# A decoder kernel: softmax left undivided until after the projection, and queries by seven products in thirty groups instead of sixteen

## The chip, the cores and the metric

The kernel runs on one core of one Trainium2 chip. TensorE (PE) multiplies matrices into PSUM[...]; VectorE (DVE) and ScalarE (ACT) read PSUM and work on SBUF; GpSimd (POOL) works on SBUF; SyncE (SP) issues most of the DMAs, ACT and POOL some. The metric is the device time of one execution in microseconds (us). Where several runs are compared, their median is given.

## The reference

Four batches of 512 rows pass through two layers, all in fp32. Most of the work, and all of the change, is in the attention of the second layer, with 16 heads of width 128, queries from the rows `x` (width 512) and keys and values from a context (width 256):

```
q = (hidden_states @ Wq).reshape(B, Sq, H, D)
k = (encoder_hidden_states @ Wk).reshape(B, Skv, H, D)
v = (encoder_hidden_states @ Wv).reshape(B, Skv, H, D)
q = rmsnorm(q, gq)
k = rmsnorm(k, gk)
scores = jnp.einsum('bqhd,bkhd->bhqk', q, k) * scale
attn = jax.nn.softmax(scores, axis=-1)
out = jnp.einsum('bhqk,bkhd->bqhd', attn, v)
out = out.reshape(B, Sq, H * D)
return out @ Wo
...
x = x + jnp.tanh(g_xattn[1]) * _L1_xattn_ref(_layernorm(x, axis=-1), ctx_1024, ...)
x = x + jnp.tanh(g_ffn[1]) * _L1_ffn_ref(_layernorm(x, axis=-1), ...)
```

Before it stand a smaller attention and a linear layer (layer 0). After it comes a layer of 16 experts, of which each row uses four; it applies to the first batch alone.

## The kernel before, in words

Layer 0 runs first, for all batches. Then the attention of the second layer runs as 64 steps, one for each head and batch: step `i` belongs to group `m = i // 2`, and a group is two heads of one batch, so there are 32 groups, eight to a batch. The experts' work for the first batch is laid into steps 22 to 56, beside the attention of later batches. I call these the expert steps.

A step has four quarters, and each begins with one score matmul: 128 queries against 512 keys (`scores`, L968). Around it `step` (from L1301) lists the other pieces of each quarter by hand:

- `keys_values` (L776) of the next group, in the even step: eight matmuls of 512 columns.
- the queries of the next group. `queries` (L858) makes a head with four matmuls of 512 columns, so eight for a group. `quarter_queries` (L881) makes both heads at once, as a 2 x 2 block product by seven block products in place of eight: fourteen matmuls of 256 columns, and sums on DVE (L896 to L918). It needs sums of blocks of `Wq` (`combine` in `load_wq`, L731 to L734, on POOL, once a group) and of the rows (`combine_rows`, L748 to L751, on DVE, once a batch). `SWITCH = (12, 28)` gives the groups that are made so.
- `values` (L1015) of the head two steps back: four matmuls of 512 columns, into the one bank psO, which ACT copies to `oT` (L1022).
- `project` (L1066): for a group, four chunks of 128 rows, each the sum over its two heads of `oT` times `wo`, so eight matmuls of 512 columns. Each chunk fills one bank (psA, psO, psT, psA), and DVE adds it to `x_sb`, times a gate (`add_to_x`, L276).

The softmax of a score tile goes: DVE multiplies by the scale of the queries and takes the row extreme (L982); ACT exponentiates and sums the rows (L983); DVE inverts the sum (L989) and multiplies the tile by it (L990), both in `share`; DVE transposes it in blocks of 32 (L261) into `tP`. After a head's fourth tile, sixteen DMAs on SP move `tP` to `big` (`move_probs`, L269), which `values` reads two steps later.

Keys take a way of their own: ACT squares them, DVE and POOL scale them (L806, L193, L810), DVE transposes blocks (L821), ACT's queue writes them to DRAM (L828) and reads them back in place (L836) as `kT`. The sums of squares of the queries go through DVE (L939), a small matmul (L947), DVE and POOL to `rq`, which L982 needs.

Each engine runs its instructions in the order of the program. That order is written by hand: a piece emits its matmuls at once, `tick()` counts them (a matmul of 512 columns is one), and `later(n, f)` emits `f` once `n` more are counted. So an instruction that waits holds up all that follows on its engine. Tiles come from pools of a few buffers in turn; PSUM has three buffers psA, two psS (scores), two psT and one psO, and a new tile waits until the last reader of the buffer's former tile is done. DMAs wait, in the same way, for the DMA that last used the same completion counter.

Of the kernel before, what the change touches and what calls it, by code (L numbers as in the profile page):

```python
# [15 lines left out]
P = 128  # L16
# [39 lines left out]
def tile_gated_decoder(  # L56
# [87 lines left out]
        nc.sync.dma_start(t[:, :, 1, :], wv_v[:, :, cols(m)])  # L144
        wkv_of[m] = t

    wqk0 = work.tile([P, G, DM], F32, tag="wo", name="wqk0")
    wq0, wk0 = (wqk0[:, a, 0 : CC * D].rearrange("p (c d) -> p c d", c=CC) for a in (0, 1))
    nc.sync.dma_start(wq0, wq0_d.rearrange("(c p) d -> p c d", p=P))
    load_ctx(0)  # L150
    nc.sync.dma_start(wk0, wk0_d.rearrange("(c p) d -> p c d", p=P))
# [71 lines left out]
        return [lambda c=c: chunk(c) for c in range(NC)], stats  # L223

    def normalised(b, c, mv, rs):
        xn = row("y", 2)
        nc.vector.tensor_scalar(
            xn, x_sb[:, b * NC + c, :], mv[:, c, 0:1], rs[:, c : c + 1], ALU.subtract, ALU.mult
        )
        return xn  # L230
# [187 lines left out]
    def layer0_attention():  # L418
# [56 lines left out]
                load_ctx(b)  # L475

        load_wq(0)()
        load_wo(0)
        load_wo(1)
        first_rows = turned_rows(0, lx1, lnt)  # L480
        for b in range(NB - 1):
            for c in range(NC):
# [224 lines left out]
    turned, moved, ends = {}, {}, {}  # L707
    n_heads = G * len(groups)

# [253 lines left out]
    def scores(i, c):  # L963


        m, h = divmod(i, G)
        sc = ps_s()
        nc.tensor.matmul(  # L968
            sc, q_of[m][h][:, c * P : (c + 1) * P], k_of[m][:, :, h, :], start=True, stop=True
        )  # L970
        st = {}

        def top():
            scale = rq_of[m][:, h * NC + c : h * NC + c + 1]

            st["e"] = row("prob", 3)
            st["den"] = col(1, "den")
# [5 lines left out]
            nc.scalar.activation(  # L983
                st["e"], st["e"], AF.Exp, bias=top, scale=-1.0, accum_out=st["den"]
            )

        def share():
            rden = col(1, "rden")
            nc.vector.reciprocal(rden, st["den"])  # L989
            nc.vector.tensor_scalar(st["e"], st["e"], rden, None, ALU.mult)  # L990
# [12 lines left out]
        later(0, top)  # L1003
        later(2, share)
        later(3, turn)

    def values(i):

        m, h = divmod(i, G)
        if h == 0:  # L1010
            o_of[m] = work.tile([P, G, S], F32, tag="oT", name="oT")
        v, oT, pT = v_of[m], o_of[m], moved.pop(i)
        po = ps_o()
        for k in range(NC):
            nc.tensor.matmul(  # L1015
                po, v[:, k, h * D : (h + 1) * D], pT[:, :, k, :], start=(k == 0), stop=(k == NC - 1)
            )
            tick()

        def copy():  # L1020

            nc.scalar.copy(  # L1022
                oT[:, h, :].rearrange("p (c g r) -> p c g r", c=NC, r=TB),
                po.rearrange("p (g c r) -> p c g r", c=NC, r=TB),
            )

        later(0, copy)
# [13 lines left out]

    def end_values(c):
        m, h = divmod(n_heads - 1, G)
        po = ps_a()
# [6 lines left out]
        later(0, lambda: nc.scalar.copy(o_of[m][:, h, c * P : (c + 1) * P], po[:, 0:P]))  # L1051

    def project(m, chunks):

        b, g = groups[m]
        oT, wo = o_of[m], wo_of[m]

        def add(t, pp):
            add_to_x(t, pp, tg[:, 1:2])
            if g == NG - 1 and b > 0:  # L1060
                nc.sync.dma_start(out_v[:, t, :], x_sb[:, t, :])

        for c in chunks:
            pp = (ps_a, ps_o, ps_t, ps_a)[c]()
            for j in range(G):
                nc.tensor.matmul(  # L1066
                    pp, oT[:, j, c * P : (c + 1) * P], wo[:, j, :], start=(j == 0), stop=(j == G - 1)
                )
# [104 lines left out]
            tick()  # L1173

    def keep_rows(s, st, table):
        y = row("y", 2)
        nc.vector.tensor_copy(y, st["py"])
        nc.sync.dma_start(table[s * P : (s + 1) * P, :], y)

# [32 lines left out]

    def rows_of(table, c, k):

        yg = row("y", 2)
# [60 lines left out]
    put(last, 3, count_over)  # L1276
    for c in range(NC):
        for k in range(TOPK):
            put(last + 1 + (c * TOPK + k) // 3, (c * TOPK + k) % 3, lambda c=c, k=k: add_row(c, k))
    for b in range(1, NB):  # L1280
        i = (b - 1) * NG * G + NG
        for j, f in enumerate(turned_rows(b, lx1, lnt)):
            put(i + j // NC * (1 + j % NC), 3 if j >= NC else j, f)
        if (b + 1) * NG > SWITCH[0]:
            put(2 * max(b * NG, SWITCH[0]) - 2, 1, lambda b=b: combine_rows(b))
        if b > 1:
            put(i, 3, lambda b=b: load_ctx(b))

# [9 lines left out]
    for c in (2, 3):  # L1298
        put(0, c - 1, lambda c=c: linear(NB - 1, turned0[NB - 1], [c]))

    def step(i):  # L1301
        m, h = divmod(i, G)
        q = m + 1
        late, late_before = by_quarters(q), by_quarters(m)
        pieces = [[], [], [], []]
        if i >= G:
            pieces[0 if i == n - 1 or h and late else 2].append(lambda: values(i - G))
        if i == n - 1:
            pieces[1].append(lambda: project(m - 1, [0, 1]))
            pieces[2] += [lambda: project(m - 1, [2, 3]), lambda: end_turn(0)]  # L1310
            pieces[3] += [lambda: values(i - 1), lambda: end_turn(1)]
            pieces[3] += [lambda: end_values(0), lambda: end_turn(2), lambda: end_values(1)]
            pieces[3] += [lambda: project(m, [0]), lambda: end_turn(3), lambda: end_values(2)]
            pieces[3] += [lambda: project(m, [1]), lambda: end_values(3)]
            pieces[3] += [lambda: project(m, [2]), lambda: project(m, [3])]
        if h == 0:
            if 0 < m < M - 1:
                pieces[0].append(lambda: keys_values(q, [0, 1]))
                pieces[1].append(lambda: keys_values(q, [2, 3]))
            if m + 2 < M:  # L1320
                pieces[2 if late else 3].append(lambda: load_wkv(m + 2))
            if m >= 2 and not late_before:
                pieces[3].append(lambda: project(m - 2, [2, 3]))
                pieces[3].append(lambda: later(4, lambda: load_wo(m)))
            if late and q < M:
                pieces[3].append(lambda: quarter_queries(q, 0))
        elif i < n - 1:
            if q < M and not late:
                pieces[0].append(lambda: queries(q, 0))
            if q < M:  # L1330
                pieces[1].append(lambda: (quarter_queries if late else queries)(q, 1))
            if m + 2 < M:
                pieces[2].append(lambda: later(6, load_wq(m + 2)))
            if late:
                pieces[2].append(lambda: project(m - 1, [0, 1]))
            if m >= 1:
                pieces[3].append(lambda: project(m - 1, [2, 3] if late else [0, 1]))
            if late and q < M:
                pieces[3].append(lambda: later(2, lambda: load_wo(q)))
            if m == 0:  # L1340
                pieces[3].append(lambda: tick(8))
        for quarter in range(4):
            if i < n:
                scores(i, quarter)
# [76 lines left out]
```

## Time and profile before

| | |
|---|---|
| median of 3 runs | 1434.96 us (1433.12 to 1439.84) |
| the profiled execution | 1437.51 us |
| its span | 1435.7 us |
| granted TensorE clock | 0.998 |
| instructions | 14871 |
| DMA | 226.99 MB, mean 158 GB/s |
| chain that ended last | PE 82%, DVE 8%, ACT 3%, DMA 2% |

In what follows a row of the timeline gives start and duration in us, the engine, the line, the operation, what it writes and reads, and how many instructions were merged; a bracket tells for how long the engine was idle before it, and what ended that. `PE` is the matmuls and `PEld` the loads of weights. A fp32 matmul appears as two records. The ends of matmuls are modelled, so the distance from one start to the next is the better measure of what one costs. A row of a group gives busy time, the mean of one in ns, and after the second bar the idle time before. A row of the windows gives busy time and count for PE, PEld, DVE, ACT and POOL, then the granted clock, the busy share of the DMA engines and GB/s.

### The profile page before, as it was taken

The numbers are of one execution on the slowest core, as the hardware profiler recorded it, in microseconds if no ns is written. First come the engines' busy times: TensorE is split into PE (matmuls) and PEld (weight loads), VectorE is DVE, ScalarE is ACT, GpSimd is POOL, SyncE is SP. The second block draws the span as 40 slices with busy tenths as digits, with TensorE's granted clock in tenths as the row PEclk, the third lists the DMA queues.
The fourth block names the chain that finished last, engine by engine and source line by source line (L and its number), as shares of the span: only waits on it lengthen the run. The fifth ranks groups of instructions, "written<-read, shape, count | busy, mean of one in ns | idle before, by whom it ended". The sixth has DMA issues, their size and how long they took to land.

```text
span 1435.7 us, 14871 instructions
## 1 busy us (share of the span) xinstructions
PE 1408.4 (98%) x3937; PEld 703.1 (49%) x3937; DVE 936.2 (65%) x2216; ACT 574.7 (40%) x1708; POOL 332.9 (23%) x274
## 2 busy tenths in 40 slices
PE   8999998999999999999999999999999999999998
PEld 4554443444444444555555555554555555544434
DVE  4778766767666677655666655566656565667774
ACT  5652224444444444333443334344334344434431
POOL 2324315322111112212221212221221222012320
PEclk9999999999999999999999999999999999999999
DMA  7533026545444445455565665656565666555652
GB/s 258 175 127 123 1 66 181 147 138 136 132 133 140 133 143 172 154 170 177 173 168 174 205 210 147 187 174 178 176 188 151 191 205 183 162 154 167 194 148 83
DMA packets 155356, 226.99 MB, mean 158 GB/s; under 512 B 24576, under 2 KB 90640, under 8 KB 155264
## 3 DMA queue, kind: packets, MB, share of 16 engines
q1 hardware_dynamic: 127312, 177.86, 42.1%
q10 hardware_dynamic: 23040, 33.56, 7.3%
q0 software_dynamic: 4912, 14.53, 3.7%
q8 instruction: 35, 0.57, 0.2%
q14 instruction: 57, 0.47, 0.1%
HBM read 129.62 MB, written 30.17 MB: 111 GB/s over the span
## 4 chain that ended last, share of the span: by engine, by line
PE 82%; DVE 8%; ACT 3%; DMA 2%; issue 1%; POOL 1%; SPq 1%; ACTq 0%; POOLq 0%
PE psA L776 15%; PE psS L968 13%; PE psO L1015 13%; PE psA L858 7%; PE psA L1066 6%; PE psA L881 5%; PE psA L1141 5%; PE psT L1066 3%; PE psO L1066 3%; PE psA L364 3%; PE psA L1169 2%; PE psA L695 1%; DMA kT<-k_d 1%; DVE x_sb L276 1%; ACT prob L983 1%
## 5 line engine op out<-in xcount | busy, mean ns | idle before, releaser
L983 ACT ACTIVATE prob<-prob,top 128x512 f32<-128x512 f32 x256 | 184.6, 721 | 562.5 <-DVE prob L982 524.1
L968 PE MATMUL psS<-kT,qT 128*128 128x512 f32 x512 | 262.3, 596 | 5.0 <-DVE x_sb L276 2.8
L776 PE MATMUL psA<-wkv,ctx 128*128 128x512 f32 x512 | 231.8, 593 | 0.3 <-ACT v L771 0.3
L1015 PE MATMUL psO<-big,v 128*128 128x512 f32 x504 | 228.9, 596 | 0.0
L982 DVE TENSOR_SCALAR_CACHE_REDUCE prob<-psS,rq 128x512 f32<-128x512 f32 x256 | 188.0, 736 | 28.9 <-PE psS L968 18.5
L989 DVE RECIPROCAL rden<-den 128x1 f32<-128x1 f32 x256 | 41.5, 162 | 242.2 <-ACT prob L983 232.9
L261 DVE STREAM_TRANSPOSE tP<-prob 128x512 f32<-128x512 f32 x252 | 178.7, 709 | 6.5
L193 POOL TENSOR_TENSOR rq<-qss,mhalf 128x8 f32<-128x8 f32 x32 | 53.4, 1668 | 485.3 <-DVE qss L955 485.3
L1015 PEld LDWEIGHTS psO<-big,v 128*128 128x128 f32 x504 | 96.0, 191 | 119.8 <-issue 115.5
L776 PEld LDWEIGHTS psA<-wkv,ctx 128*128 128x128 f32 x512 | 96.3, 190 | 118.1 <-issue 109.6
L990 DVE TENSOR_SCALAR prob<-prob,rden 128x512 f32<-128x512 f32 x256 | 141.3, 552 | 9.0
L968 PEld LDWEIGHTS psS<-kT,qT 128*128 128x128 f32 x512 | 92.9, 190 | 79.6 <-issue 62.0
L193 POOL TENSOR_TENSOR rk<-kss,mhalf 128x8 f32<-128x8 f32 x32 | 52.8, 1650 | 319.3 <-DVE kss L806 319.2
L1066 PE MATMUL psA<-wo,oT 128*128 128x512 f32 x256 | 121.1, 594 | 2.2 <-ACT oT L1022 2.2
L858 PE MATMUL psA<-lnT,wq 128*128 128x512 f32 x256 | 115.6, 592 | 0.0
L1141 PE MATMUL psA<-gu,xgT 128*128 128x352 f32 x272 | 86.0, 459 | 0.0
L821 DVE STREAM_TRANSPOSE tK<-kn 128x256 f32<-128x256 f32 x128 | 45.4, 411 | 55.3 <-POOL kn L810 55.3
L1066 PEld LDWEIGHTS psA<-wo,oT 128*128 128x128 f32 x256 | 48.1, 190 | 64.2 <-issue 54.4
L858 PEld LDWEIGHTS psA<-lnT,wq 128*128 128x128 f32 x256 | 48.3, 190 | 59.3 <-issue 59.3
L796 ACT ACTIVATE ksq<-kn 128x128 f32<-128x128 f32 x256 | 75.2, 298 | 0.0
L1141 PEld LDWEIGHTS psA<-gu,xgT 128*128 128x128 f32 x272 | 51.7, 190 | 37.9 <-issue 15.5
L276 DVE SCALAR_TENSOR_TENSOR x_sb<-psA,tg,x_sb 128x512 f32<-128x512 f32 x80 | 58.2, 727 | 6.7 <-PE psA L695 3.8
(197 smaller groups left out, 1811.5 us busy)
## 6 DMA issues: line engine op xcount, KB each, us to landing
big<-tP SPq DMA_DIRECT2D x1008, 64.0 KB
k_d<-tK ACTq DMA_DIRECT2D x32, 512.0 KB
kT<-k_d ACTq DMA_DIRECT2D x128, 128.0 KB
wq<-in_wq_dram SPq DMA_DIRECT2D x32, 512.0 KB
wo<-in_wo_dram SPq DMA_DIRECT2D x32, 512.0 KB
gu<-in_gate_dram SPq DMA_DIRECT2D x16, 704.0 KB
gu<-in_up_dram SPq DMA_DIRECT2D x16, 704.0 KB
wkv<-in_wk_dram SPq DMA_DIRECT2D x32, 256.0 KB
```

Source lines behind the costliest of these rows:

```text
L193: nc.gpsimd.tensor_tensor(out, v, mhalf[:, :n], ALU.pow)
L261: nc.vector.transpose(tP[:, :, c, :], e.rearrange("p (j r) -> p j r", r=TB))
L776: nc.tensor.matmul(pp, ctxs[b][:, k, c * P : (c + 1) * P], wkv[:, k, :, :].rearrange("p a n -> p (a n)"), start=(k == 0), stop=(k == CC - 1),)
L796: nc.scalar.activation(sq[:, c, at], kn[:, c, at], AF.Square, accum_out=st["kss"][:, c * G + h : c * G + h + 1],)
L858: nc.tensor.matmul(pp, wq[:, k, h * D : (h + 1) * D], lx1[b][:, k, :], start=(k == 0), stop=(k == KC - 1))
L968: nc.tensor.matmul(sc, q_of[m][h][:, c * P : (c + 1) * P], k_of[m][:, :, h, :], start=True, stop=True)
L982: nc.vector.tensor_scalar(e, x, scale, 3.0e38, ALU.mult, ALU.min, accum_out=top)
L983: nc.scalar.activation(st["e"], st["e"], AF.Exp, bias=top, scale=-1.0, accum_out=st["den"])
L990: nc.vector.tensor_scalar(st["e"], st["e"], rden, None, ALU.mult)
L1015: nc.tensor.matmul(po, v[:, k, h * D : (h + 1) * D], pT[:, :, k, :], start=(k == 0), stop=(k == NC - 1))
L1066: nc.tensor.matmul(pp, oT[:, j, c * P : (c + 1) * P], wo[:, j, :], start=(j == 0), stop=(j == G - 1))
L1141: nc.tensor.matmul(st[a][:, :FF], st["xgT"][:, k * P : (k + 1) * P], st["gu"][:, a, k, :], start=(k == 0), stop=(k == KC - 1),)
```

## The change

It has two parts, and moves pieces around them.

The exponentials are not divided any more. `den` becomes a column of `dens`, one tile of four columns for a head; when its four tiles are through, `part` takes the four reciprocals at once and multiplies by the gate, which gives `share_of[i]`. `project` now works on one head and one chunk: a single matmul, whose result is added to `x_sb` times `share_of[i]` where it was `tg` before. The last two heads are still divided and projected together.

`SWITCH` becomes `(2, 32)`: the queries of groups 2 to 31 are made by `quarter_queries`.

To this belongs: `wo` and `oT` are held and loaded by head; `project` of head `i - 3` runs in step `i`, one chunk a quarter; `values` is always in quarter 2; the second half of `quarter_queries` moves to quarter 0 in steps without experts; `combine` for the weights runs in quarter 1 of the following step and no longer six ticks after the load is issued; the gathered rows of the experts come four to a step from step 57 on, with three buffers `y`, and are added six ticks later, not ten; and the last step has a new order.

```diff
-SWITCH = (12, 28)
+SWITCH = (2, 32)
...
-        xn = row("y", 2)
+        xn = row("y", 3)
...
-    def load_wo(m):
-        g = groups[m][1]
-        t = work.tile([P, G, DM], F32, tag="wo", name="wo")
-        nc.sync.dma_start(t, wo_v[:, g * G : (g + 1) * G, :])
-        wo_of[m] = t
+    def load_wo(i):
+        wo_of[i] = row("wo", 4)
+        nc.sync.dma_start(wo_of[i], wo_v[:, i % H, :])
...
+        if c == 0:
+            den_of[i] = col(NC, "dens", 6)
...
         def share():
             rden = col(1, "rden")
-            nc.vector.reciprocal(rden, st["den"])
+            nc.vector.reciprocal(rden, den_of[i][:, c : c + 1])
             nc.vector.tensor_scalar(st["e"], st["e"], rden, None, ALU.mult)
+
+        def part():
+
+            share_of[i] = col(NC, "share", 6)
+            nc.vector.reciprocal(share_of[i], den_of[i])
+            nc.vector.tensor_scalar(share_of[i], share_of[i], tg[:, 1:2], None, ALU.mult)
...
         later(0, top)
-        later(2, share)
+        if i >= n_heads - G:
+            later(2, share)
         later(3, turn)
+        if i < n_heads - G and c == NC - 1:
+            later(6, part)
...
-        for c in chunks:
-            pp = (ps_a, ps_o, ps_t, ps_a)[c]()
-            for j in range(G):
-                nc.tensor.matmul(
-                    pp, oT[:, j, c * P : (c + 1) * P], wo[:, j, :], start=(j == 0), stop=(j == G - 1)
-                )
-                tick()
-            later(1, lambda t=b * NC + c, pp=pp: add(t, pp))
+    def project(i, c, bank):
+
+        b, own = i // H, [i] if i < n_heads - G else [i, i + 1]
+        pp = bank()
+        for j in own:
+            nc.tensor.matmul(
+                pp, o_of[j][:, c * P : (c + 1) * P], wo_of[j], start=(j == i), stop=(j == own[-1])
+            )
+            tick()
+
+        def add():
+            add_to_x(b * NC + c, pp, share_of[i][:, c : c + 1] if len(own) == 1 else tg[:, 1:2])
...
-        later(10, add)
+        later(6, add)
...
-            put(last + 1 + (c * TOPK + k) // 3, (c * TOPK + k) % 3, lambda c=c, k=k: add_row(c, k))
+            put(last + 1 + c, k, lambda c=c, k=k: add_row(c, k))
...
+        at = 1 if not late or first <= i < last else 0
         pieces = [[], [], [], []]
+        v_at = 2
+        if i > G:
+            for c in range(NC):
+                bank = ps_t if c == v_at else ps_a if c == 3 or c == 1 and not first <= i <= last else ps_o
+                pieces[c].append(lambda c=c, bank=bank: project(i - G - 1, c, bank))
         if i >= G:
-            pieces[0 if i == n - 1 or h and late else 2].append(lambda: values(i - G))
+            pieces[v_at if i < n - 1 else 3].append(lambda: values(i - G))
+        if G < i < n - 1:
+            pieces[3].append(lambda: later(4, lambda: load_wo(i + 1)))
...
         if h == 0:
+            while combine_wq:
+                pieces[1].append(combine_wq.pop())
...
             if q < M:
-                pieces[1].append(lambda: (quarter_queries if late else queries)(q, 1))
+                pieces[at].append(lambda: (quarter_queries if late else queries)(q, 1))
             if m + 2 < M:
-                pieces[2].append(lambda: later(6, load_wq(m + 2)))
-            if late:
-                pieces[2].append(lambda: project(m - 1, [0, 1]))
-            if m >= 1:
-                pieces[3].append(lambda: project(m - 1, [2, 3] if late else [0, 1]))
-            if late and q < M:
-                pieces[3].append(lambda: later(2, lambda: load_wo(q)))
+                pieces[1 + at].append(lambda: combine_wq.append(load_wq(m + 2)))
```

More of the change, by code (lines that the diff above doesn't have):

```diff
@@ L145, in load_wkv @@
         wkv_of[m] = t
-    wqk0 = work.tile([P, G, DM], F32, tag="wo", name="wqk0")
-    wq0, wk0 = (wqk0[:, a, 0 : CC * D].rearrange("p (c d) -> p c d", c=CC) for a in (0, 1))
+    wq0, wk0 = (
+        row("wo", 4)[:, 0 : CC * D].rearrange("p (c d) -> p c d", c=CC) for a in (0, 1)
+    )
     nc.sync.dma_start(wq0, wq0_d.rearrange("(c p) d -> p c d", p=P))
@@ L477, in layer0_attention @@
         load_wq(0)()
-        load_wo(0)
-        load_wo(1)
+        for i in range(4):
+            load_wo(i)
         first_rows = turned_rows(0, lx1, lnt)
@@ L706, in tile_gated_decoder @@
     q_of, sq_of, lxs_of, halves, rq_of, kn_of, k_of, v_of, o_of = {}, {}, {}, {}, {}, {}, {}, {}, {}
-    turned, moved, ends = {}, {}, {}
+    turned, moved, ends, den_of, share_of = {}, {}, {}, {}, {}
     n_heads = G * len(groups)
@@ L976, in top @@
             st["e"] = row("prob", 3)
-            st["den"] = col(1, "den")
+            den = den_of[i][:, c : c + 1]
             e, x, top = st["e"], sc, col(1, "top")
@@ L983, in top @@
             nc.scalar.activation(
-                st["e"], st["e"], AF.Exp, bias=top, scale=-1.0, accum_out=st["den"]
+                st["e"], st["e"], AF.Exp, bias=top, scale=-1.0, accum_out=den
             )
@@ L1003, in scores @@
         later(0, top)
-        later(2, share)
+        if i >= n_heads - G:
+            later(2, share)
         later(3, turn)
+        if i < n_heads - G and c == NC - 1:
+            later(6, part)
     def values(i):
         m, h = divmod(i, G)
-        if h == 0:
-            o_of[m] = work.tile([P, G, S], F32, tag="oT", name="oT")
-        v, oT, pT = v_of[m], o_of[m], moved.pop(i)
+        o_of[i] = row("oT", 3)
+        v, oT, pT = v_of[m], o_of[i], moved.pop(i)
         po = ps_o()
@@ L1022, in copy @@
             nc.scalar.copy(
-                oT[:, h, :].rearrange("p (c g r) -> p c g r", c=NC, r=TB),
+                oT.rearrange("p (c g r) -> p c g r", c=NC, r=TB),
                 po.rearrange("p (g c r) -> p c g r", c=NC, r=TB),
@@ L1043, in end_values @@
         m, h = divmod(n_heads - 1, G)
-        po = ps_a()
+        if c == 0:
+            o_of[n_heads - 1] = row("oT", 3)
+        oT, po = o_of[n_heads - 1], ps_a()
         for k in range(NC):
@@ L1050, in end_values @@
         tick(1)
[L1051 to L1061, printed above, removed]
-        for c in chunks:
-            pp = (ps_a, ps_o, ps_t, ps_a)[c]()
-            for j in range(G):
-                nc.tensor.matmul(
-                    pp, oT[:, j, c * P : (c + 1) * P], wo[:, j, :], start=(j == 0), stop=(j == G - 1)
-                )
-                tick()
-            later(1, lambda t=b * NC + c, pp=pp: add(t, pp))
+        later(0, lambda: nc.scalar.copy(oT[:, c * P : (c + 1) * P], po[:, 0:P]))
+    def project(i, c, bank):
[4 more added lines that the diff above has]
+                pp, o_of[j][:, c * P : (c + 1) * P], wo_of[j], start=(j == i), stop=(j == own[-1])
+            )
+            tick()
+        def add():
+            add_to_x(b * NC + c, pp, share_of[i][:, c : c + 1] if len(own) == 1 else tg[:, 1:2])
+            if own[-1] % H == H - 1 and b > 0:
+                nc.sync.dma_start(out_v[:, b * NC + c, :], x_sb[:, b * NC + c, :])
+        later(1, add)
     gate_v = gate_d.rearrange("e i n -> (e i) n")
@@ L1175, in keep_rows @@
     def keep_rows(s, st, table):
-        y = row("y", 2)
+        y = row("y", 3)
         nc.vector.tensor_copy(y, st["py"])
@@ L1213, in rows_of @@
     def rows_of(table, c, k):
-        yg = row("y", 2)
+        yg = row("y", 3)
         nc.gpsimd.indirect_dma_start(
@@ L1278, in tile_gated_decoder @@
         for k in range(TOPK):
-            put(last + 1 + (c * TOPK + k) // 3, (c * TOPK + k) % 3, lambda c=c, k=k: add_row(c, k))
+            put(last + 1 + c, k, lambda c=c, k=k: add_row(c, k))
+    for b in range(NB):
+        if (b + 1) * NG > SWITCH[0]:
+            put(2 * max(b * NG, SWITCH[0]) - 2, 1, lambda b=b: combine_rows(b))
     for b in range(1, NB):
@@ L1283, in tile_gated_decoder @@
             put(i + j // NC * (1 + j % NC), 3 if j >= NC else j, f)
-        if (b + 1) * NG > SWITCH[0]:
-            put(2 * max(b * NG, SWITCH[0]) - 2, 1, lambda b=b: combine_rows(b))
         if b > 1:
@@ L1299, in tile_gated_decoder @@
         put(0, c - 1, lambda c=c: linear(NB - 1, turned0[NB - 1], [c]))
+    combine_wq = []
     def step(i):
@@ L1303, in step @@
         q = m + 1
-        late, late_before = by_quarters(q), by_quarters(m)
+        late = by_quarters(q)
+        at = 1 if not late or first <= i < last else 0
         pieces = [[], [], [], []]
+        v_at = 2
[3 more added lines that the diff above has]
+                pieces[c].append(lambda c=c, bank=bank: project(i - G - 1, c, bank))
         if i >= G:
-            pieces[0 if i == n - 1 or h and late else 2].append(lambda: values(i - G))
+            pieces[v_at if i < n - 1 else 3].append(lambda: values(i - G))
+        if G < i < n - 1:
+            pieces[3].append(lambda: later(4, lambda: load_wo(i + 1)))
         if i == n - 1:
[L1309 to L1315, printed above, removed]
+            at_end = [
+                lambda: end_turn(0), lambda: project(i - G, 0, ps_a), lambda: end_turn(1),
+                lambda: project(i - G, 1, ps_o), lambda: end_values(0), lambda: end_turn(2),
+                lambda: project(i - G, 2, ps_t), lambda: end_values(1), lambda: end_turn(3),
+                lambda: project(i - G, 3, ps_a), lambda: end_values(2), lambda: values(i - 1),
+                lambda: end_values(3),
+            ]
+            pieces[3] += at_end + [
+                lambda c=c, bank=bank: project(i - 1, c, bank)
+                for c, bank in enumerate((ps_a, ps_o, ps_t, ps_a))
+            ]
         if h == 0:
+            while combine_wq:
+                pieces[1].append(combine_wq.pop())
             if 0 < m < M - 1:
@@ L1321, in step @@
                 pieces[2 if late else 3].append(lambda: load_wkv(m + 2))
-            if m >= 2 and not late_before:
-                pieces[3].append(lambda: project(m - 2, [2, 3]))
-                pieces[3].append(lambda: later(4, lambda: load_wo(m)))
             if late and q < M:
@@ L1342, in step @@
         for quarter in range(4):
-            if i < n:
-                scores(i, quarter)
+            scores(i, quarter)
             more = extra.get((i, quarter), [])
```

## The prediction

> **What bounds the kernel now.** I read the page's busy shares first, then TensorE's waits, then its timeline in one group of each kind. A group is two steps, an even one (the keys and values of the next group are made) and an odd one.
>
> ```profile
> PE 1408.4 (98%) x3937; PEld 703.1 (49%) x3937; DVE 936.2 (65%) x2216; ACT 574.7 (40%) x1708; POOL 332.9 (23%) x274
> ```
>
> TensorE is busy for 98% of the span. Matmul ends are modelled, so this alone proves little; its list of waits does:
>
> ```profile
> PE psT L245 <- DVE y L227: 4.7, 7, 1.1
> PE psA L285 <- DMA ctx<-in_ctxT_dram: 4.6, 1, 4.6
> PE psS L968 <- DVE x_sb L276: 2.8, 1, 2.8
> PE psA L1169 <- ACT hT L1162: 2.5, 2, 1.5
> PE psA L1066 <- ACT oT L1022: 2.2, 2, 1.7
> PE psS L968 <- DMA kT<-k_d: 2.1, 1, 2.1
> ```
>
> The columns are total us, times, longest. With the small ones left out TensorE waits some 22 us in 1435.7, all at a few places: the start, 208 to 246 us, six steps that turn rows, 1382 to 1391 us. In an ordinary group it waits for nobody. So only TensorE's own time counts, as long as the others keep up.
>
> **Seven products.** Sizes come from starts, not from the modelled durations. A fp32 matmul is two records. First a plain group, then one by quarters:
>
> ```profile
> 473.62 3.60 PE L858 MATMUL psA<-lnT,wq 128*128 128x512 f32 x8
> 477.05 1.02 PE L968 MATMUL psS<-kT,qT 128*128 128x512 f32 x2
> ```
>
> ```profile
> 796.07 1.03 PE L881 MATMUL psA<-lnT,wq 128*128 128x256 f32 x4
> 796.94 1.03 PE L881 MATMUL psA<-lxs,wqs 128*128 128x256 f32 x4
> 797.80 1.03 PE L881 MATMUL psA<-lxs,wq 128*128 128x256 f32 x4
> 798.66 1.03 PE L881 MATMUL psA<-lxs,wqs 128*128 128x256 f32 x4
> 799.53 1.02 PE L968 MATMUL psS<-kT,qT 128*128 128x512 f32 x2
> ```
>
> Eight records of 512 columns take 477.05 - 473.62 = 3.43 us (429 ns each), sixteen of 256 take 799.53 - 796.07 = 3.46 us (216 ns each). A plain group spends 16 x 0.429 = 6.86 us on its queries, seven products 28 x 0.216 = 6.05 us: 0.81 less. The window of groups grows from 12-27 to 2-31, by 14: **-11.3 us**.
>
> A rule speaks against this. The Trainium skill ("TensorE: Matmul & The Clock Gate", Back-to-back issue gap) says that in a real stream of weight loads and matmuls the spacing is 81 ns at 128 columns and 131 at 512, so that narrow matmuls pay more than their share. A straight line between puts 256 columns at 98 ns, 75% of 512; seven products would then cost 14/8 x 0.75 = 1.31 times the plain form, +2.1 us a group and +29 us (an estimate). The rows above come from this kernel and give 216/429 = 50%, because the load (190 ns) fits under even a half-width pass. I take the row.
>
> What it adds elsewhere, per group: DVE five sums of 0.41 us (L896 to L918); POOL four sums of 0.74 (L731 to L734); ACT two copies of 0.36 and 0.14 for scaling in SBUF. Fourteen times: DVE 29 us, POOL 41, ACT 12; and one more combining of rows, 2.7 us of DVE in step 2, needed two quarters later. POOL is 23% busy; its sums now start a step after the load was issued, and are needed two quarters later. Free.
>
> **Undivided exponentials.**
>
> ```profile
> L989 DVE RECIPROCAL rden<-den 128x1 f32<-128x1 f32 x256 | 41.5, 162 | 242.2 <-ACT prob L983 232.9
> L990 DVE TENSOR_SCALAR prob<-prob,rden 128x512 f32<-128x512 f32 x256 | 141.3, 552 | 9.0
> L276 DVE SCALAR_TENSOR_TENSOR x_sb<-psA,tg,x_sb 128x512 f32<-128x512 f32 x80 | 58.2, 727 | 6.7 <-PE psA L695 3.8
> ```
>
> 62 of 64 heads lose four pairs: 248 x (0.162 + 0.552) = -177 us of DVE. Projection by head makes 252 additions where there were 128: 124 x 0.727 = +90. A share per head (a reciprocal and a product of 128x4, about 0.16 + 0.22 by L989 and the 128x4 rows of L333): 62 x 0.38 = +24. Net -63 us, with the seven products -32: DVE falls to about 904 us. By itself this is worth nothing, since DVE did not hold TensorE; it pays for the sums of the seven products. TensorE has the same 256 projection matmuls, but each now fills a bank alone, so 124 more drains stand between a bank and its next user. `wo` comes in 64 loads of half the size; SP has one more issue a group (0.4 us) beside 32 moves of 0.63, 23 us in a group of 34; the load of `wq` is issued a quarter earlier in odd steps without experts, behind the same moves: free. At the very end the first projection follows the copy of `oT` (0.59 us) over 0.44 us of transposes: some 0.4 us, left out.
>
> **The balance of the steps** is what changes. Before, odd steps took 17.3 us without experts and 19.5 with:
>
> ```profile
> 472.76:490.10 17.34, 17.34 (x43) 7.82 (x42) 13.40 (x32) 5.97 (x13) 0.69 (x2) 1.00 0.60 181
> 799.53:818.98 19.45, 19.45 (x56) 10.00 (x55) 13.31 (x32) 7.27 (x19) 1.68 (x1) 1.00 0.66 206
> ```
>
> (The fourth number but for the counts is DVE: 13.4 and 13.3 us.) After, an odd step without experts holds scores 3.43, one head's projection 3.43, values 3.43, the last three products 2.6 and the row sums 0.14: 13.0 us; the even one 20.6. DVE has in the odd one four row maxima (0.82), transposes (0.71) and additions (0.73), four sums (1.6), the reduction of squares (1.25) and small ones (0.9): 12.8 us, of which pipelining takes some 0.9. It just fits; over the group it is 24 of 34. Four places have little slack:
>
> (a) Keys. `kT` must be back before the next even step.
>
> ```profile
> 477.40 0.36 ACTq L828 DMA_DIRECT2D k_d<-tK  x1
> 480.42 0.90 ACTq L836 DMA_DIRECT2D kT<-k_d  x2
> 481.35 2.17 ACTq L836 DMA_DIRECT2D kT<-k_d  x2
> 483.57 0.60 ACT L864 ACTIVATE sq<-psA 128x512 f32<-128x512 f32 x1 [2.40 <-DMA big<-tP]
> ```
>
> By the packets of ACT's queue `kT` lands 7.6 to 9.2 us after L828 issues in plain groups, and is needed 12.7 after. L828 keeps its distance from the keys' matmuls (13.2 us), which is now 2.9 us into the odd step, so 10.1 are left. Issues of L836 wait for moves of `big` (the bracket in the last row). Moves are 0.63 us apart and land 2.9 us after issue (at 806.86, group 17, the last L836 waited for the fifth, issued at 804.0). They now start about 1.7 us before the odd step; the last L836 goes by the 14th, at -1.7 + 13 x 0.63 + 2.9 = 9.4; `kT` lands some 2.2 later, at 11.6, against 13.0: 1.4 us early. Late are groups that took longer: 12.7 (group 2, beside the gathers of step 2), 10.3 (group 3), 12.2 (group 31), together 4.9 us. Group 2 waits 2.1 already: **+2.8 us** (0 to 26, if all 13 groups without experts are 2 us late).
>
> (b) psO in odd expert steps: the bank is used by the projection of quarter 0 and again by that of quarter 1, 1.2 us after. DVE does L899, L900, the share, a row maximum and then the addition: from 0.2 us into the step 0.36 + 0.36 + 0.4 + 0.74 + 0.75 = 2.8 us, against 2.9 when TensorE wants it. Between 0 and 0.4 a group; I take 0.15, as the pipelined spacing of the rows is behind these: 17 x 0.15 = **+2.5 us** (0 to 7).
>
> (c) `hT` behind the issues of L836 and one exponential: ready at about 6.9, wanted at 7.2. Free; 0.5 us late in each of 17 groups would be 8.
>
> (d) The waits for `y` and for the last additions (4.7 + 2.8 us) come from a late DVE, which has 0.7 us less per score and 0.7 more per new addition, and four gathered rows a step at the end in place of three. Between -5 and +5; I take half of the first: **-2.5 us**.
>
> Sum against the profiled execution: 1437.5 - 11.3 + 2.8 + 2.5 - 2.5 = 1429.0 us. That execution is 2.55 above the median of the runs, so against the median: **1426 us**, -0.6%.
>
> **Rivals.**
>
> *Stalls shrink too.* A lighter DVE lets TensorE through at 208 to 246 us, at the turned rows and at the end; (a) and (b) cost nothing. For it: every wait of L245 and the 2.8 us is DVE's. Against: two of the early ones are ACT and DMA. 11.3 + 6 less: 1418.
>
> *Given back.* The odd steps, one quarter shorter, cost 0.3 us in each of 30 groups, from any of (a) to (c): 9 us back, 1433. For it: three chains within half a microsecond. Against: no ordinary group waits now.
>
> *Slower: the keys come late.* Place: the score matmul that opens each even step without experts. Price: what `kT` lands after 10.1 us from L828. If DVE, full in the odd step, starts the moves 3 us later, every L836 behind them slips as much and all but 1.4 us shows: 13 x 1.6 = 21; with the exponentials and the `oT` copy behind L836 on ACT another 0.5 in 30 groups, 15. 1435 - 11 + 36 = 1460; a mild form 1445. It decides from 0.87 us a group (11.3/13), and is measurably slower from 1.4. For it: groups 2 and 31 already need over 12 us. Against: the other groups need under 9.2, and DVE's transposes no longer wait for the division.
>
> That the matmuls are not saved is no rival: their number in the program is what the diff says (112 of 512 columns fewer, 196 of 256 more).
>
> **Chances.** Forecast 0.50 (1420 to 1431 by itself), shrinking stalls 0.13, given back 0.14, late keys 0.23. A measurement tells about 0.5% from no change here, 7.2 us: faster is under 1427.8, slower over 1442.1. Faster: 0.42 of the forecast's half and the first rival, 0.55. Same: the rest of the forecast, giving back, and 0.03 of late keys, 0.25. Slower: 0.20. The range goes from 1417 to 1445.
>
> **What would show it.** TensorE's L858 group falls from 256 records to 32 and L881 rises from 448 to 840, at 216 ns between starts; L990 falls to 8; DVE is near 904 us. Right if TensorE's waits stay near 22 us in all. Wrong if `psS <- DMA kT` recurs in many groups (a), `psO <- DVE x_sb` (b), `psA <- ACT hT` (c), or if 256-column matmuls space out beyond 216 ns in the short steps.

## The result, and the profile after

The changed kernel takes 1445.35 us (median of 17 runs, 1439.93 to 1450.89), the kernel before 1436.82 beside it (17 runs, 1433.12 to 1440.39): a ratio of 1.0057, 95% interval 1.0047 to 1.0068. Forecast was 1426, faster. It is slower, by 0.57%, a little more than the 0.5% that the prediction took for what a measurement can tell from no change. The profiled execution took 1448.22 us with a span of 1446.5 (1435.7 before), at a granted clock of 0.992.

The page's row of engines, then the rows of L881 by operand, which stand for the seven products (duration min/median/max, first and last start):

```profile
PE 1404.5 (97%) x4105; PEld 736.5 (51%) x4105; DVE 905.1 (63%) x2042; ACT 594.6 (41%) x1736; POOL 373.9 (26%) x330
```

```profile
L881 PE MATMUL psA<-lnT,wq x240: 379/379/379, 223.5 to 1380.8; 128*128 128x256 f32 x120
L881 PE MATMUL psA<-lxs,wqs x240: 379/379/379, 224.3 to 1378.2; 128*128 128x256 f32 x120
L881 PE MATMUL psA<-lxs,wq x240: 379/379/382, 225.2 to 1381.6; 128*128 128x256 f32 x120
L881 PE MATMUL psA<-lnT,wqs x120: 379/379/454, 230.3 to 1384.7; 128*128 128x256 f32 x120
```

The work is what was foreseen: 240 + 240 + 240 + 120 = 840 records of L881, whose starts lie 216 ns apart in the median, and DVE at 905 us against a forecast of 904. If each matmul is given the median distance between starts for its shape, TensorE has 11.4 us less to do than before. But what its starts lie apart beyond that, its waits and slow stretches, grew from 28.3 us to 50.5. The difference, +22.2 - 11.4 = +10.8, is the longer span.

TensorE's waits in the changed kernel (total us, times, longest):

```profile
PE psS L971 <- DMA kT<-k_d: 11.8, 4, 6.1
...
PE psS L971 <- DVE x_sb L277: 3.3, 2, 2.1
PE psS L971 <- DVE prob L985: 2.5, 3, 1.2
PE psS L971 <- ACT prob L986: 2.5, 2, 1.4
...
PE psT L246 <- DVE y L228: 1.8, 3, 1.1
```

`kT` leads the list with 11.8 us where it had 2.1. The list says less than there is, though. Three more rows are score matmuls that wait by name for DVE or ACT, and most of these are the same matmul at the same place, the one that opens an even step without experts. By the distance of starts this one matmul loses 2.3 us before (group 2 alone) and 20.3 us after, in nine groups: 2 (6.2), 3 (3.1), 5 (1.4), 6 (1.3), 7 (2.2), 10 (0.9), 29 (1.3), 30 (2.3) and 31 (1.6). In all of them the last packet of `kT` ends 0.8 to 1.4 us before the matmul starts, whatever releaser the list names.

The late keys cost more than the wait. At three of the nine places (groups 2, 3 and 7) the granted clock falls to 0.5 for 6.8, 6.8 and 3.4 us, during the wait or within 1.3 us of its end. Group 3, the matmuls and a window of that stretch:

```profile
285.19 2.04 PE L971 MATMUL psS<-kT,qT 128*128 128x512 f32 x2 [2.96 <-DMA kT<-k_d]
...
288.73 4.86 PE L776 MATMUL psA<-wkv,ctx 128*128 128x512 f32 x8
293.43 1.02 PE L971 MATMUL psS<-kT,qT 128*128 128x512 f32 x2
...
295.14 3.60 PE L776 MATMUL psA<-wkv,ctx 128*128 128x512 f32 x8
298.58 1.02 PE L971 MATMUL psS<-kT,qT 128*128 128x512 f32 x2
```

```profile
284.40:291.20 6.80, 6.01 (x7) 2.52 (x8) 3.36 (x8) 1.33 (x4) 4.62 (x6) 0.50 0.09 23
```

The eight records of L776 take 293.43 - 288.73 = 4.70 us there, in the next quarter 3.44. In the three stretches the matmuls come 6.9 us later in all than at their median distances, and that is on top of the 20.3 us. Why the clock fell at these three places and not at the other six is not shown. The kernel before has one such stretch while matmuls run, near its end, of 3.4 us; it cost 1.7 us.

How ACT's order looks around the keys of group 6 in the changed kernel, to set beside the rows of group 9 shown for before (477.40 to 483.57). `ACTq` is the issue of a DMA; it holds ACT's order for as long as the row says, and a row of several counts the waits between them too:

```profile
381.16 0.34 ACTq L828 DMA_DIRECT2D k_d<-tK  x1
...
384.84 0.31 ACTq L836 DMA_DIRECT2D kT<-k_d  x1
385.01 0.71 ACT L922 ACTIVATE qT<-qT,gqk 128x512 f32<-128x512 f32 x1
385.26 2.90 ACTq L836 DMA_DIRECT2D kT<-k_d  x3
388.21 0.72 ACT L986 ACTIVATE prob<-prob,top 128x512 f32<-128x512 f32 x1 [2.49 <-DMA kT<-k_d]
```

From the start of the last three issues to their end 2.90 us pass, and ACT is idle for 2.49 us before the exponential behind them. The chain of waits over the same stretch (start, us, what; rows of 0.03 us and less left out) follows from there into the next group:

```profile
385.26 2.95 DMA kT<-k_d
388.21 0.81 ACT prob L986 x2
389.05 0.71 DVE tP L262
389.76 0.63 DVE x_sb L277
...
391.52 0.67 DVE prob L985 x2
392.21 0.82 ACT prob L986 x2
393.07 1.10 PE psS L971 x2
```

There is no TensorE in it up to the score matmul at 393.07: the step is no longer bound by matmuls. This chain runs through exponential, transpose, addition and row maximum, while the packets of `kT` end at 392.1. Which of the two holds the matmul can't be read here; an experiment has to say.

The windows of even and odd steps of two groups (busy us and count for PE, PEld, DVE, ACT, POOL; then clock, DMA share, GB/s) show the cost beside an undisturbed group:

```profile
357.12:378.25 21.13, 21.13 (x60) 11.11 (x61) 12.04 (x26) 10.43 (x37) 9.15 (x8) 1.00 0.44 99
378.25:393.07 14.82, 13.72 (x43) 7.29 (x42) 12.18 (x29) 6.96 (x15) 1.47 (x1) 1.00 0.67 190
465.50:486.12 20.62, 20.62 (x57) 10.64 (x56) 11.81 (x27) 9.96 (x36) 7.58 (x7) 1.00 0.35 93
486.12:499.23 13.11, 13.11 (x39) 7.06 (x38) 10.05 (x24) 5.72 (x12) 0.00 (x0) 1.00 0.73 215
```

The second pair has 20.62 + 13.11 = 33.73 us, 0.83 less than the 34.56 of a group before: there the change pays as worked out. (The first pair turns rows too, which is 0.88 us of TensorE more.) In the shorter odd step the DMA engines are busy for 0.67 to 0.73, and for 0.60 in the odd step shown of before: the moves are the same, the time is less. This share alone does not tell which keys are late: the late ones of group 6 come in the step at 0.67, the timely ones of group 9 in that at 0.73.

By place, the 10.8 us of span are: start to group 2, -0.1; groups 2 to 10, +8.7; groups 11 to 27, -5.1; groups 28 to 30, +5.7; the last group and the end, +1.5. So the groups that were to gain lost 14 us, and the expert steps, where I saw a loss of 2.5 at psO, gained 5.

### The profile page after: what moved, and what is told of

It is laid out like the page before. It is cut to its first block, busy times and chain, and to the rows that moved or that the text cites. A ratio compares the mean times of both kernels' runs of the same rounds, so it can differ in the third digit from the quotient of the medians.

```text
span 1446.5 us, 15324 instructions
## 1 busy us (share of the span) xinstructions
PE 1404.5 (97%) x4105; PEld 736.5 (51%) x4105; DVE 905.1 (63%) x2042; ACT 594.6 (41%) x1736; POOL 373.9 (26%) x330
## 4 chain that ended last, share of the span: by engine, by line
PE 78%; DVE 7%; DMA 5%; SPq 3%; ACT 2%; issue 2%; POOL 1%; ACTq 0%; DVEq 0%; POOLq 0%
PE psA L776 15%; PE psS L971 12%; PE psO L1026 11%; PE psA L881 9%; PE psO L1071 5%; PE psA L1152 5%; PE psA L1071 4%; PE psA L1180 3%; PE psT L1071 3%; SPq L270 3%; PE psA L365 3%; DMA kT<-k_d 2%; DMA big<-tP 2%; PE psA L696 1%; ACT prob L986 1%
## 5 line engine op out<-in xcount | busy, mean ns | idle before, releaser
L971 PE MATMUL psS<-kT,qT 128*128 128x512 f32 x512 | 265.1, 600 | 20.2 <-DMA kT<-k_d 11.8
L776 PE MATMUL psA<-wkv,ctx 128*128 128x512 f32 x512 | 234.2, 598 | 0.0
L776 PEld LDWEIGHTS psA<-wkv,ctx 128*128 128x128 f32 x512 | 97.9, 193 | 120.4 <-issue 111.7
L1071 PE MATMUL psO<-wo,oT 128*128 128x512 f32 x198 | 104.5, 611 | 1.6 <-DVE prob L985 1.6
L1071 PE MATMUL psA<-wo,oT 128*128 128x512 f32 x186 | 95.4, 596 | 2.2 <-ACT oT L1033 2.2
L770 ACT COPY kn<-psA 128x256 f32<-128x256 f32 x128 | 47.7, 373 | 92.6 <-PE psA L776 90.7
L1033 ACT COPY oT<-psO 128x512 f32<-128x512 f32 x63 | 36.8, 583 | 96.3 <-PE psO L1026 96.2
L277 DVE SCALAR_TENSOR_TENSOR x_sb<-psO,share,x_sb 128x512 f32<-128x512 f32 x97 | 70.9, 731 | 4.0 <-PE psO L1071 2.2
L277 DVE SCALAR_TENSOR_TENSOR x_sb<-psA,share,x_sb 128x512 f32<-128x512 f32 x89 | 66.1, 743 | 5.1 <-PE psA L1071 1.7
L1071 PE MATMUL psT<-wo,oT 128*128 128x512 f32 x128 | 65.2, 592 | 0.0
```

The costliest lines, as they stand in the source:

```text
L277: nc.vector.scalar_tensor_tensor(x_sb[:, t, :], src, gate, x_sb[:, t, :], ALU.mult, ALU.add)
L776: nc.tensor.matmul(pp, ctxs[b][:, k, c * P : (c + 1) * P], wkv[:, k, :, :].rearrange("p a n -> p (a n)"), start=(k == 0), stop=(k == CC - 1),)
L971: nc.tensor.matmul(sc, q_of[m][h][:, c * P : (c + 1) * P], k_of[m][:, :, h, :], start=True, stop=True)
L1071: nc.tensor.matmul(pp, o_of[j][:, c * P : (c + 1) * P], wo_of[j], start=(j == i), stop=(j == own[-1]))
```

## The experiments

Theory **K**: the keys come late (the slower rival of the prediction). Theory **D**: DVE, filled up in the odd steps, holds TensorE. Later ones carry a letter in their expectations. All ratios are to the kernel before on the same chip, whose median was 1436.0 to 1438.5 there, so ratios say more than times.

**1. Nobody waits for late keys.** The scores of all groups use the keys of group 0; the others are still made, written and read back.

```diff
-            kT = work.tile([P, NT, G, P], F32, tag="kT", name="kT")
+            kT = work.tile([P, NT, G, P], F32, tag="kT" if m else "kT0", bufs=1, name="kT")
...
-            sc, q_of[m][h][:, c * P : (c + 1) * P], k_of[m][:, :, h, :], start=True, stop=True
+            sc, q_of[m][h][:, c * P : (c + 1) * P], k_of[0][:, :, h, :], start=True, stop=True
```

> All scores are taken with the keys of group 0; the keys of every group are still made, written out and read back, but no matmul waits for them, so the output is not the reference's. Theory K (the keys come back too late for the short odd steps): the waits of TensorE at the opening score of the even steps without experts, some 20 us in the changed kernel, go, and with them as much time: 1424 to 1429 us; what stays is the waits of the first steps for oT and of the last steps. Rival D (DVE, full in the odd step, hands over the queries, maxima or drains too late, and the keys only happen to be as late): the waits stay under another name, 1441 to 1447 us.

1429.3 us, ratio 0.9947 (0.9928 to 0.9965): 16 us less than the changed kernel. Its longest waits:

```profile
PE psA L286 <- DMA ctx<-in_ctxT_dram: 5.4, 1, 5.4
PE psA L881 <- DVE share L998: 4.5, 2, 2.5
PE psA L776 <- ACT v L771: 2.6, 2, 1.8
```

`kT` is gone from the list, and so are `x_sb` and ACT's `prob` as releasers of scores. All score matmuls at the opening of even steps are on time, and groups 3 to 10 take 33.73 us each (34.61 where rows are turned). ACT's issues still hold up its exponentials in this kernel (2.52 us in group 6, at 377.78 us); so of the two chains above it was the key tile that held the score. K holds, with its size: some 16 of the 19 us by which the forecast was off. The half clock behind late openings is gone with them (the first such stretch comes at 1404 us). Not all of the loss comes back, because other waits show in its place: group 2 still takes 37.50 us and group 30 37.75.

**2 and 3. The two parts of the change apart.** First undivided exponentials and projection by head, with seven products as before the change:

```diff
-SWITCH = (2, 32)
+SWITCH = (12, 28)
```

> Undivided exponentials and projection by head, seven products only in groups 12 to 27. Theory K: odd steps without experts last 17 us again, so the keys are in time and no even step waits; TensorE's matmuls are those of before, and the last steps still wait for gathered rows: 1436 to 1441 us. Rival P (a projection matmul alone in its bank, with 124 more drains, costs TensorE waits): it stays at 1443 us or above, with waits on DVE x_sb.

1435.14 us, ratio 0.9992 (0.9984 to 0.9999), DVE 876 us. That is just under K's range; but two openings are still late (groups 2 and 30, 5.7 us together), where K had none. By itself the part is worth next to nothing, and costs nothing.

Then seven products for groups 2 to 31 in the kernel before, with division and the old steps; `combine_rows` is also called for the first batch:

```diff
-SWITCH = (12, 28)
+SWITCH = (2, 32)
...
+    for b in range(NB):
+        if (b + 1) * NG > SWITCH[0]:
+            put(2 * max(b * NG, SWITCH[0]) - 2, 1, lambda b=b: combine_rows(b))
```

> The kernel before with seven products in groups 2 to 31, its division, projection by group and order of pieces kept: an odd step without experts then holds scores 3.4, values 3.4, three products 2.6 and two projections 6.9, 16.4 us. Theory K: the keys are in time, and the 11.3 us of matmuls are gained: 1425 to 1431 us. Rival D: DVE carries 29 us more of sums and all divisions (some 965 us), it falls behind in steps of 17 us and TensorE waits: 1437 us or above.

1477.29 us, ratio 1.028 (1.026 to 1.030), in D's range, a miss for K and for my picture of it. The first waits of this kernel:

```profile
PE psT L245 <- DVE y L227: 11.5, 9, 3.2
PE psA L776 <- DVE x_sb L276: 11.1, 7, 3.2
PE psT L947 <- DVE part L939: 9.2, 7, 2.6
PE psA L776 <- ACT v L771: 8.4, 2, 6.4
PE psS L968 <- DVE prob L982: 7.2, 3, 5.0
```

Four of five are DVE's, with DVE busy for 953 us or 64%: hardly more than the 936 of before. Groups 1 to 10 and 28 to 30 lose 40 of the 44 us of span, and the granted clock is at 0.5 for 34 us of this execution. So a share of busy time far from full doesn't say that DVE can take the sums: with the division, the groups without experts had no place for them. The changed kernel, with no division, is 32 us faster than this one; but it also moves pieces, and what share of the 32 us belongs to the division alone is not shown.

**4. Balance.** If the first half of the seven products moves from the even step into the odd one, the odd step is 3.4 us longer and the keys have 12.7 us from L828 in place of 10.7 (10.1 was foreseen).

```diff
-        at = 1 if not late or first <= i < last else 0
+        inner = first <= i < last
+        at = 1
...
-            if late and q < M:
+            if late and q < M and inner:
                 pieces[3].append(lambda: quarter_queries(q, 0))
...
+            if q < M and late and not inner:
+                pieces[0].append(lambda: quarter_queries(q, 0))
```

> The changed kernel with the first half of the seven products moved from the end of the even step to the start of the odd one, in steps without experts alone: even 17.2, odd 16.5 us. Theory K: the keys get 3.5 us more, the waits at the even steps go but for group 2's, 1426 to 1432 us. Rival D: DVE has the same work in a longer odd step but more of it there (sums of both halves), waits only move: 1440 to 1447 us.

1440.57 us, ratio 1.0029 (1.0021 to 1.0038). The time is D's, the trace is half K's: of the late scores only group 2's is left (5.4 us by the distance of starts), groups 3 to 9 take 33.7 to 34.8 us, but groups 10, 29 and 30 lengthen to 36.5, 38.8 and 37.2:

```profile
PE psS L971 <- DMA kT<-k_d: 5.2, 1, 5.2
PE psA L881 <- DVE u L896: 5.1, 3, 2.2
```

The three waits for `u`, at 546, 1334 and 1372 us, are seven products that meet a DVE behind with other work. DVE waited there for rows itself: 2.9 us for the experts' rows (`xn_d`) in the first case, 2.1 us for a gathered row in each of the others.

**5 and 6. Rows at the end.** In the last steps of the changed kernel DVE waits for a gathered row (the bracket), and TensorE's `psA L881` waits behind it:

```profile
1344.00 0.75 DVE L277 SCALAR_TENSOR_TENSOR x_sb<-y,tw,x_sb 128x512 f32<-128x512 f32 x1 [2.59 <-DMA y<-y_d,posi]
```

So the rows as they were, in the changed kernel, and then with experiment 1 too:

```diff
-        later(6, add)
+        later(10, add)
...
-            put(last + 1 + c, k, lambda c=c, k=k: add_row(c, k))
+            put(last + 1 + (c * TOPK + k) // 3, (c * TOPK + k) % 3, lambda c=c, k=k: add_row(c, k))
```

> The kernel after, with the gathered rows at the end as before: three issued a step instead of four, each added ten ticks after its issue instead of six. Theory E (about 5 us of the loss is the vector engine waiting for gathered rows near the end): 1438 to 1441 us, the idle time of the vector engine before L277 for y at 1344 us gone, TensorE's psA L881 waits in the last steps shorter. Rival W (the last steps lose time to the extra sums and additions themselves, wherever the rows are added): 1443 to 1447, the same waits at the end.

1444.73 us, ratio 1.0053 (1.0036 to 1.0070). In the profiled execution groups 29 and 30 are 3.8 us shorter, but the runs show no gain that could be told from none: E missed, and the time is in W's range.

> Both suspected causes taken away: all scores multiply by the keys of group 0 (the other groups' keys are still made, sent and brought back; the attention weights are then those of the wrong keys), and the gathered rows as before. If late keys (16 us by the run with group 0's keys alone, 1429.3) and rows (5 us) add up: 1422 to 1426, some 22 us under the kernel after and close to before less 14 groups of 0.81. If the rows were only late because of the keys' delays, or the end loses to its own work (W): 1428 to 1431.

1425.32 us, ratio 0.9914 (0.9900 to 0.9929), in the foreseen 1422 to 1426. Beside experiment 1 that is 4.0 us less, with intervals that just touch; groups 28 to 30 now take 33.73 us each (36.66 and 37.75 for the latter two in experiment 1). So the rows probably cost some 4 us once the keys are on time, and little while they are late. How the two hide each other I did not follow up.

**7 and 8. Why the keys are late.** The four loads (L836) issued from POOL's queue instead of ACT's: first for all groups, in the changed kernel; then only for groups 4 to 10 and 29 to 31, with rows as before.

```diff
-                nc.scalar.dma_start(
+                nc.gpsimd.dma_start(
```

> The kernel after, with the four loads that bring the keys back issued from POOL's queue instead of ACT's. Theory Q (the keys are late because the four issues stand in ACT's order behind exponentials, copies and waits for moves): the keys land within 9 us of L828 in most groups, 1430 to 1436 us. Rival S (they are late because the packets run beside the 32 moves, or because the write before them is slow): landing at 10 to 12 us after L828 as in the kernel after, 1442 to 1448; the same time also if POOL's own sums hold the issues up.

1455.42 us, ratio 1.0122 (1.0105 to 1.0140). Neither range. Groups 3 to 9, where the keys were late, take 33.73 to 33.81 us (35.01 in one of those that turn rows); the loss is concentrated:

```profile
PE psS L971 <- DMA kT<-k_d: 19.9, 5, 9.3
```

Group 2's loads are issued 9.2 us after L828 and group 11's 12.6, against 3.2 to 4.7 in most. Groups 29 and 30 also wait 5.7 us for DVE's `share` (L881). POOL's order around group 11 shows what its loads stand behind: a gather that itself waits for `xn_d`.

```profile
560.74 1.10 POOL L1132 DMA_INDIRECT xg<-xn_d,rowi  x1 [14.49 <-DMA xn_d<-y]
562.87 2.24 POOL L836 DMA_DIRECT2D kT<-k_d  x4 [1.03 <-issue]
```

The selective form leaves those groups with ACT:

```diff
-                nc.scalar.dma_start(
+                (nc.gpsimd if 4 <= m <= 10 or m > 28 else nc.scalar).dma_start(
```

> The kernel after with rows at the end as before, and the loads of the keys issued from POOL only for groups 4 to 10 and 29 to 31; group 2's, 3's and 11's, which stood on POOL behind gathers, stay with ACT. Theory Q (ACT's order makes the keys of ordinary groups late): 1431 to 1436 us, no wait of a score matmul for kT in groups 4 to 10. Rival S (transport): 1441 or more, as the kernel with the old rows alone, 1444.7.

1435.03 us, ratio 0.9982 (0.9973 to 0.9991), as Q foresaw, 10 us under the same kernel with ACT's queue (experiment 5). Groups 4 to 10 open on time. The keys of group 6 and the chain of waits from there on, to set beside those of the changed kernel:

```profile
379.79 0.33 ACTq L828 DMA_DIRECT2D k_d<-tK  x1
...
384.27 0.71 ACT L986 ACTIVATE prob<-prob,top 128x512 f32<-128x512 f32 x1
```

```profile
383.54 2.28 POOL L836 DMA_DIRECT2D kT<-k_d  x4 [7.98 <-PE psA L1071]
```

```profile
385.23 3.43 PE psO L1026 x8
388.66 0.14 PE psT L947 x2
388.80 0.94 PE psS L971 x2
389.74 0.86 PE psA L1071 x2
```

The four issues take 2.28 us and stand in nobody's way; ACT's exponential follows at once (no bracket), and the chain is matmuls alone. The last issue comes 5.7 us after L828 in the median of groups 4 to 10 (6.7 with ACT's queue in the changed kernel), the last packet after 8.7 (10.3). Of the 1.6 us, 1.0 is the earlier issue.

The edit changes more than the order, though. The DMA queues around the keys of group 6 (packets, MB, share), in the changed kernel (381.0 to 393.6 us) and here (379.5 to 390.4):

```profile
q10 hardware_dynamic: 720, 1.05, 26.8%
```

```profile
q0 software_dynamic: 192, 0.52, 21.1%
q10 hardware_dynamic: 144, 0.52, 12.9%
```

The write of the keys is 144 packets. The same 0.52 MB of loads came in 576 packets from ACT's queue (data in pieces of 1 KB) and in 192 from POOL's (4 KB). So Q's range was met, but the order of issue and the form of the packets changed together, and no run takes them apart. Nor is every place cured: group 30, also on POOL's queue, still opens 2.2 us late.

**9 to 12. Which version is best.** Seven products only for groups 4 to 28 spare group 2 and the end. With rows as before: with balance (experiment 4), with neither, and with POOL's queue as in experiment 8.

```diff
-SWITCH = (2, 32)
+SWITCH = (4, 29)
```

> A version meant to keep the gain: the kernel after with the first quarter's query products in the odd step (so the odd step stays long and the keys have time), rows at the end as before, and seven products only for groups 4 to 28. 25 groups instead of 16 save 9 x 0.81 = 7.3 us. Theory K (late keys and the end's rows are all that was lost): 1427 to 1432 us. Rival D (the vector engine, filled up in the odd step, gives back what TensorE saves): 1434 to 1440, with TensorE waiting at psA L881 for u or share in many groups.

1430.07 us, ratio 0.9953 (0.9939 to 0.9968), in K's range.

> The version for groups 4 to 28 without its balance: the first quarter's query products are in the even step again, as in the kernel after. Theory K: the keys are late again in groups 4 to 10, 1435 to 1441 us. Rival N (the version won only because groups 2, 3 and 29 to 31 went back to plain queries): 1429 to 1432, the same as with the balance.

1437.14 us, ratio 0.9997 (0.9985 to 1.0008), K's: the late keys are back, 12.5 us of late score matmuls in seven groups. So the version did not win by its smaller window.

> Seven products for groups 4 to 28, steps as in the kernel after, keys of groups 4 to 10 and 29 to 31 loaded from POOL's queue. Theory Q: as good as the balanced version or a little better, 1427 to 1431 us. Rival S: like the same kernel with ACT's queue, 1435 to 1441.

1429.31 us, ratio 0.9939 (0.9922 to 0.9956), Q's. One edit, from which queue four loads are issued, is worth 8 us here; all else in the program is the same, but the packets of the loads are not (experiment 8). Last, balance and rows for groups 2 to 31:

> The balanced version with seven products for groups 2 to 31 again, rows at the end as before. If only late keys and the end's rows were lost (theory K alone): 1425 to 1429 us, five groups at 0.81 better than the version for groups 4 to 28. If seven products cost more than they save where other work already fills the vector engine (groups 2, 3 and 29 to 31, theory D there): 1433 to 1438.

1439.42 us, ratio 1.0018 (1.0010 to 1.0025), above both ranges. The trace still has 6.5 us of waits for `kT`, and 5.3 for DVE's `part`. Five groups at 0.81 us, which the window takes in, cost 9 where they meet the gathers of group 2 and the end.

The two good versions, with intervals that overlap, are the best found: 0.5 to 0.6% faster than the kernel before.

## Why the prediction was wrong

**Seven products: right.** -11.3 us was foreseen, -11.4 is in the starts of the matmuls; 256 columns stay at 216 ns in the short steps too. The row of the trace was the right choice over the rule, by which the estimate was +29.

**Undivided exponentials: right**, with DVE at 905 us and nothing gained or lost alone (experiment 2). That they pay for the sums was a clause; experiment 3 shows what the sums cost without them.

**(a) Keys: the step that failed.** I had the mechanism, the place, even the form of the loss as a rival at 0.23, and gave it +2.8 us. Measured: 20.3 - 2.3 = +18.0 at the opening score matmuls, and 6.9 more at half clock behind three of them, a cost that the prediction did not have. In the prediction "the last L836 goes by the 14th, at -1.7 + 13 x 0.63 + 2.9 = 9.4; `kT` lands some 2.2 later, at 11.6, against 13.0: 1.4 us early". The moves did start 1.7 us before the odd step (in groups 4 to 10), so the reason that the slower rival gave, moves 3 us late, is not what happened. The odd step did become 13.1 us. In terms of L828 the last issue was to be at 6.5, the landing at 8.7, the need at 10.1. In the 13 groups whose keys come in an odd step without experts (2 to 11 and 29 to 31) the last issue is at 6.7 in the median (4.9 to 9.3): that term was good. Two others were not. The landing comes 3.8 us after the last issue in the median (1.9 to 5.1), not 2.2, which holds for the kernel before (2.3). And a score matmul starts 0.8 to 1.4 us after the last packet, which I counted as nothing. A third was too strict: most groups have 10.7 us from L828, not 10.1. With the landing at 10.3 in the median and 0.9 more to the matmul, that leaves 10.7 - 10.3 - 0.9 = -0.5 us where 1.4 was foreseen. I had named only the groups that were over 10.1 *before*, and not asked what the same moves, pressed into a step four microseconds shorter, do to the others. That this pressing is what makes the landing longer is likely, but not shown. Experiment 8 shows that loads from POOL's queue make ordinary groups punctual; whether by the order of issue alone stays open.

**(b) psO: foreseen +2.5 in ordinary expert steps, measured nothing there.** An odd expert step of 16.03 us and an even one of 25.79 make 41.82, the 41.81 of before. The wait shows only in two odd steps that turn rows, 25 and 41:

```profile
PE psO L1071 <- DVE prob L985: 1.6, 2, 0.8
```

**(c) hT: nothing lost**, as said; its two waits of before (2.5 us) are gone, which was not foreseen.

**(d) Additions: right in the middle, wrong at the end.** The waits for `y` fell from 4.7 us to 1.8, where I took 2.5 off. With those for `hT` gone and those for psO added, the six groups that turn rows among the expert steps (12 to 14, 20 to 22) are 4.8 us shorter in all. But at the end I saw "four gathered rows a step" only as a part of a span from -5 to +5; added six ticks after the issue they are waited for (experiments 5 and 6, some 4 us if the keys are on time).

**The offset** of 2.55 us between the profiled execution and the median rested on three runs; with 17 the median is 1436.82 and the offset 0.7.

So the forecast of the sum fails by one term. (a) is 18.0 + 6.9 = 24.9 us in place of 2.8, 22 us too much; all the rest together came nearly 3 us better than foreseen, and the profiled execution is 19 us off. The range's upper end, 1445, was the mild form of that rival, and the median fell just beyond it.

## What to carry to other kernels

A slack is a difference of two times, and both ends need their tails: add what lies between the last packet and the instruction that uses it, and ask what the same transfers take when the step in which they run becomes shorter. When work is moved from one step to its neighbour, look at the transfers whose deadline is the boundary; an even split can be worth more than fewer matmuls. A wait of TensorE can cost more than its length: look at the granted clock behind it. DMA issues that wait hold up all behind them on their queue: put them on the engine that has least to do *at that time*, not on average, and look whether the packets stay the same.

## What the runs showed of the hardware

The same four issues, in the same group beside the same moves, from ACT's queue and from POOL's (duration of one in ns, min/median/max; first and last start):

```profile
L836 ACTq DMA_DIRECT2D kT<-k_d x4: 310/325/587, 384.8 to 387.8; - x4
L836 POOL DMA_DIRECT2D kT<-k_d x4: 553/553/635, 383.5 to 385.3; - x4
```

One issue took longer on POOL, yet the four were through in 2.28 us there and in 3.3 on ACT: on ACT some 1.8 us of that were gaps, in which by the semaphores of the trace the queue waited for moves of `big` to land. The time from the last packet of a load to the start of a matmul that waited for it was 0.8 to 1.4 us in all nine places. Behind three of these nine waits the granted clock was 0.5 for 3.4 to 6.8 us, and records of 512 columns started 0.85 us apart in place of 0.43.
